# Self-attention logits from the normalised rows and one product of both weights, in a fused attention and feed-forward block

## The chip, the cores and the metric

The kernel runs on one core of a Trainium2 chip. A core has five engines that run side by side and meet at semaphores: TensorE (PE, matrix products into PSUM), VectorE (DVE), ScalarE (ACT), GpSimd (POOL) and SyncE (SP), which issues DMAs. ScalarE and GpSimd issue DMAs as well. The metric is the device time of one execution in microseconds; shown is the median of several runs. One further execution is recorded by the hardware profiler; its span runs from the first to the last instruction.

## The reference

There are 8 batches. `x` is [8, 128, 512], the context is [8, 2048, 384], everything is float32. Three layers follow one another, each added to `x`; a layer norm without gain stands ahead of each.

```python
x = x + xattn(layernorm(x), ctx)       # 8 heads of 64, 2048 context rows
x = x + attn(layernorm(x))             # one head of 512
x = x + ffn(layernorm(x))              # 512 -> 2048 -> 512, quantised

# attn(y), the layer that the change touches
queries = y @ Wq + bq
keys    = y @ Wk + bk
values  = y @ Wv + bv
logits  = einsum('bik,bjk->bij', queries, keys)
logits  = where(j > i, -inf, logits)
probs   = softmax(logits, axis=1) / sqrt(512)     # over the queries i
read    = einsum('bij,bjv->biv', probs, values)
return y + read
```

The softmax runs over the queries, and the layer adds its own input, the normalised rows, to its result. With y_i the row of the query and y_j that of the key, a logit is

```
(y_i Wq + bq) . (y_j Wk + bk) = y_i . (y_j Wk Wq^T + Wq bk) + y_j . (Wk bq) + bq . bk
```

so it can be formed from the rows themselves, the product Wk Wq^T (512 x 512), the vectors Wq bk and Wk bq, and one number.

## The kernel before

The kernel keeps tiles with 128 partitions. Rows and weights of 512 lie in NK = 4 blocks of 128. The 8 batches of the later layers are two groups of GB = 4, so that a matmul can move GT = 512 columns.

**Order of the work.** TensorE's order is the order of the source throughout (L136). So is ScalarE's and VectorE's (L242, L244) until `first.close()` and `in_turn.close()` at L781 and L782, in the first step of the last batch. What comes after that on VectorE and ScalarE, and all of GpSimd's and SyncE's work, DMA issues included, is put in order by a planner: it simulates the program, and lets an engine take the instruction that is ready and stands first in the source. A later instruction can so be placed well ahead of an earlier one that is not ready yet. A tile that takes over the buffer of an older tile waits until all readers and writers of the older one are done, DMAs among them.

**Prologue.** The first 56 us form the keys of batch 0's first half by plain matmuls, the layer norm of all rows for the cross-attention (`q_norm`), its queries (`q_proj`, kept in DRAM) and sums of context blocks and of weight blocks (`sum_half`, `sum_w`) for a block product that needs 20 matmul units in place of 24 (`block_product`, L286). `keep_rows` (L454) adds the bias `bo` to the rows on GpSimd and stores them. Then come `k_proj(0, 0, (1,))` and `v_proj(0, 0)` (L714, L715). `block_product` is a generator that stops twice on the way, so that other work can be set between its parts.

**Main loop.** For each batch b and step m of 4 (two heads a step): `scores(b, m)` (16 matmuls; VectorE copies them out of PSUM with a running maximum, L483), `attend` of the step before, a `unit` of other matmuls, the exponentials (L497), the 32 x 32 transposes on VectorE and 16 DMAs that finish the transposition (`turns`, L502 to L513). The `unit` forms keys and values for the next batch; in the last batch there is no next one, and it forms the self-attention of group 0: the queries in step 1 (L741), the keys in step 2 (L743), the weights in step 3. The tile of values for the second half, `v_proj(b, 1)`, has the tag "v1" in the pool `vp`; for batch 0 it is first written in step 0, by the ScalarE copy at L300.

**Self-attention.** `enter_self_attention` (L675) frees the context's tiles and loads the weights and biases on GpSimd's queue. The class `SelfAttention` (L587 on) has for each row block: `norm` (L597; statistics and scaling on VectorE, the square root on ScalarE, the addition to the residual on GpSimd, L124), `turn` (L600; four TensorE transposes and a ScalarE copy into `xt`), `turned_rows` (L603; queries or keys, [512 features, 512 rows], 16 matmuls in the source and 32 instructions in the profile, evicted by ScalarE with the bias, L613), `weights` (L623; logits with the key on the partition, mask, softmax), `values` and `read`. Group 0 is normalised and turned at the end of step 0 of the last batch (L785 to L787). Group 1 follows behind the loop (L790 to L804, L869 to L877).

**Feed-forward.** `quantize_w2` (L816) rounds w2 to a small format on VectorE, `hidden` (L831) forms and rounds the hidden rows, `output` and `finish` (L854, L861) the result.

## Time and profile before

| | |
|---|---|
| time, median of 3 runs | 1126.11 us (1125.96 to 1127.3) |
| time of the profiled execution | 1125.29 us |
| its span | 1123.5 us |
| mean granted TensorE clock | 0.997 |
| TensorE busy | 1107.7 us |
| VectorE busy | 823.3 us |
| ScalarE busy | 338.0 us |
| GpSimd busy | 233.2 us |
| `psq` (queries) of group 0, start to end | 847.1 to 861.1 us |
| `psq` and `psk` of group 1, start of the first to start of the logits | 922.95 to 952.21 us |
| last matmul of the kernel ends | 1115.9 us |

Times in the profile are microseconds from the start of the span. A line of the timeline gives the start, the length, the engine, the source line, the instruction, "written<-read" by tile names, the shape, how many instructions were merged (x32), and in brackets the idle time just before and what ended it. Matmuls are pipelined: the length of one overlaps the next, so the spacing of starts is what counts. A float32 matmul of 512 columns appears as two instructions. PEld are TensorE's weight loads beside the matmuls; SPq are DMA issues on SyncE's queue. In a table of DMA issues the last number is the median time from issue to landing.

### The profile page before, as it was taken

Reading aid. Unit: us, or ns where it says so; the run is one execution under the profiler, and the core shown is the slowest. Engines: PE = TensorE matmul, PEld = TensorE weight load, DVE = VectorE, ACT = ScalarE, POOL = GpSimd, SP = SyncE. Lnnn points to the kernel's source line nnn. Section 1 sums busy time; section 2 is a strip of 40 time slices with the busy share of each in tenths; the row PEclk is TensorE's granted clock in tenths of the full one; section 3 lists DMA queues with packets and bytes.
Section 4 is the critical chain, followed back from the end, with each engine's and each line's share of the span. In section 5 each row is a group of like instructions: output and inputs, shape, how many; then the busy total and the mean of one; then the engine's idle time right before and its main releaser. Section 6 shows DMA issues by size and latency. Waiting matters only on the chain.

```text
span 1123.5 us, 16786 instructions
## 1 busy us (share of the span) xinstructions
PE 1107.7 (99%) x6286; PEld 833.9 (74%) x6286; DVE 823.3 (73%) x1710; ACT 338.0 (30%) x531; POOL 233.2 (21%) x322
## 2 busy tenths in 40 slices
PE   9999999999999999999999999999999999999997
PEld 5487778788878877787888788777865544687775
DVE  5947777777767777777777677777795559767777
ACT  3323223233322222232333222222343322232221
POOL 0404401520450044006204500440030000000001
PEclk9999999999999999999999999999999999999999
DMA  8415535534654455355346544543383473000001
GB/s 290 177 50 129 132 76 141 150 76 92 156 146 100 108 141 142 78 138 151 75 94 156 136 101 101 151 126 76 89 259 75 109 239 113 1 1 20 10 10 38
DMA packets 48497, 125.12 MB, mean 111 GB/s; under 512 B 10384, under 2 KB 15520, under 8 KB 47520
## 3 DMA queue, kind: packets, MB, share of 16 engines
q1 hardware_dynamic: 46192, 117.48, 40.5%
q0 software_dynamic: 1360, 5.78, 1.6%
q8 instruction: 50, 0.82, 0.3%
q10 hardware_dynamic: 864, 0.79, 0.2%
q14 instruction: 31, 0.25, 0.1%
HBM read 49.03 MB, written 7.86 MB: 51 GB/s over the span
## 4 chain that ended last, share of the span: by engine, by line
PE 95%; DVE 3%; ACT 1%; issue 0%; DMA 0%; DVEq 0%; ACTq 0%
PE pv_z L403 21%; PE pk_z L380 19%; PE po L524 10%; PE sc L479 10%; PE ph L847 9%; PE pv_b L403 4%; PE pk_b L380 3%; PE psq L609 3%; PE psk L609 2%; PE py L562 2%; PE psv L650 2%; PE pq L447 2%; PE pf L856 2%; PE k L362 2%; PE pl L628 1%; DVE p L483 0%
## 5 line engine op out<-in xcount | busy, mean ns | idle before, releaser
L497 ACT ACTIVATE p<-p,nm 128x2048 f32<-128x2048 f32 x64 | 128.2, 2003 | 427.7 <-DVE nm L491 311.1
L510 DVE STREAM_TRANSPOSE p<-p 128x512 f32<-128x512 f32 x256 | 158.9, 679 | 84.0 <-ACT p L497 83.9
L483 DVE TENSOR_SCALAR_CACHE_REDUCE p<-sc 128x512 f32<-128x512 f32 x256 | 159.0, 686 | 29.5 <-PE sc L479 28.9
L403 PE MATMUL pv_z<-wv_sums,x 128*128 128x256 f32 x640 | 157.9, 382 | 0.0
L205 POOL TENSOR_TENSOR m<-x 128x256 f32<-128x256 f32 x70 | 51.1, 730 | 513.1 <-DMA x<-in_ctx_t_dram 467.1
L380 PE MATMUL pk_z<-x,wk_sums 128*128 128x256 f32 x600 | 149.7, 382 | 0.8 <-ACT kt L300 0.6
L403 PEld LDWEIGHTS pv_z<-wv_sums,x 128*128 128x128 f32 x640 | 120.6, 190 | 18.0 <-issue 1.5
L524 PEld LDWEIGHTS po<-pT,v 128*64 128x64 f32 x2048 | 111.2, 137 | 24.6 <-issue 21.5
L380 PEld LDWEIGHTS pk_z<-x,wk_sums 128*128 128x128 f32 x600 | 112.7, 190 | 19.8 <-issue 2.9
L479 PE MATMUL sc<-kt,q 64*128 64x512 f32 x512 | 119.9, 603 | 2.5 <-DVE p L483 2.5
L524 PE MATMUL po<-pT,v 128*64 128x128 f32 x2048 | 118.9, 274 | 0.3 <-issue 0.3
L847 PE MATMUL ph<-xf,w 128*128 128x256 f32 x512 | 111.3, 379 | 0.0
L403 PE MATMUL pv_z<-wv_sums,m 128*128 128x256 f32 x448 | 107.5, 380 | 0.2 <-ACT v L300 0.2
L847 PEld LDWEIGHTS ph<-xf,w 128*128 128x128 f32 x512 | 97.4, 190 | 13.7 <-issue 0.5
L380 PE MATMUL pk_z<-m,wk_sums 128*128 128x256 f32 x420 | 101.4, 380 | 0.0
L479 PEld LDWEIGHTS sc<-kt,q 64*128 64x128 f32 x512 | 47.3, 187 | 62.3 <-issue 53.6
L403 PEld LDWEIGHTS pv_z<-wv_sums,m 128*128 128x128 f32 x448 | 83.4, 190 | 13.0 <-issue 0.8
L380 PEld LDWEIGHTS pk_z<-m,wk_sums 128*128 128x128 f32 x420 | 79.2, 190 | 11.7 <-DVE kt L303 0.4
L300 ACT COPY v<-pv_z 128x512 f32<-128x512 f32 x112 | 62.8, 589 | 58.9 <-PE pv_z L403 58.9
L300 ACT COPY kt<-pk_z 128x512 f32<-128x512 f32 (+1 forms) x112 | 59.7, 558 | 58.0 <-PE pk_z L380 57.5
L205 POOL TENSOR_TENSOR x<-x 128x256 f32<-128x256 f32 x98 | 69.8, 730 | 0.8 <-DMA x<-in_ctx_t_dram 0.8
L303 DVE TENSOR_TENSOR v<-pv_z,v 128x512 f32<-128x512 f32 x96 | 63.2, 685 | 5.2 <-PE pv_z L403 5.2
(171 smaller groups left out, 1223.2 us busy)
## 6 DMA issues: line engine op xcount, KB each, us to landing
pT<-p SPq DMA_DIRECT2D x512, 128.0 KB, 2.4
x<-in_ctx_t_dram SPq DMA_DIRECT2D x45, 512.0 KB, 5.6
w<-in_w_t_dram SPq DMA_DIRECT2D x1, 4096.0 KB, 13.2
w2f<-in_w_t_dram SPq DMA_DIRECT2D x16, 256.0 KB, 2.7
x_in<-in_x_dram SPq DMA_DIRECT2D x8, 256.0 KB, 6.7
xd<-x_in SPq DMA_DIRECT2D x2, 1024.0 KB, 4.3
qd<-xq SPq DMA_DIRECT2D x8, 256.0 KB, 4.5
q<-qd SPq DMA_DIRECT2D x8, 256.0 KB, 3.3
```

Source lines behind the costliest of these rows:

```text
L205: eng.tensor_tensor(x_block(b, h, to), x_block(b, h, one), x_block(b, h, two), ALU.add if op == "+" else ALU.subtract,)
L300: nc.scalar.copy(outs[ij], views(ps))
L303: nc.vector.tensor_tensor(outs[to], views(ps), outs[other], op)
L380: nc.tensor.matmul(ps[:, ts(i, BK)], wk_sums[:, WSLOT[WAT[r]], f2, :], x_block(b, h, XAT[r]), start=start and i == 0, stop=True, skip_grou ...
L403: nc.tensor.matmul(ps[:, ts(t, 256)], x[:, ts(t, P)], wv_sums[:, WSLOT[WAT[r]], :], start=start and t == 0, stop=True, skip_group_check=True,)
L479: nc.tensor.matmul(pair[i], q[r, :], kts[b, m // 2][r, m % 2, ts(n, 512)], start=True, stop=True)
L483: nc.vector.tensor_scalar(p[:, :, i].rearrange("p g (t i) -> p t g i", i=SQ)[:, ts(n, Q)], pair[i].rearrange("p (t g i) -> p t g i", g=Q, ...
L497: nc.scalar.activation(p[:, :, i], p[:, :, i], AF.Exp, bias=nms[b, m][:, i : i + 1], scale=SCALE, accum_out=sums[b][:, h : h + 1],)
L510: nc.vector.transpose(p[:, g, i], p[:, g, i])
L524: nc.tensor.matmul(pos[b][h * DH : (h + 1) * DH, ts(m, P)].rearrange("p (a i) -> p a i", a=Q), v[:, jt % 8, ts(2 * m + h, DH)], turned_[b, ...
L609: nc.tensor.matmul(ps, weight[:, k, ts(m, P)], self.xt[:, k, :], start=(k == 0), stop=(k == NK - 1),)
L847: nc.tensor.matmul(ps[:, :n], w1[:, k, ts(c, P)], xt[:, k, at], start=(k == 0), stop=(k == NK - 1),)
```

## The change

The logits are formed from the rows. In place of queries and keys of each group there is `both`, the product Wk Wq^T, formed once by TensorE (`both_weights`, 16 matmuls in the source) in the last batch's step 1, and `keys(both)`, the rows times this product plus Wq bk (16 matmuls per group). The logits are these keys against the normalised rows `xt`. The part y_j . (Wk bq) + bq . bk, a number per key row, is formed on VectorE for each row block in `norm` (a product with the row `u` = Wk bq, summed along the row) and enters where the mask was added.

The product needs both weights with their columns on the partitions. They are turned in the prologue: both weights are loaded into a tile `w_sa` of the tag "v1", VectorE forms Wq bk and Wk bq from them (eight products summed along the row) and transposes them in place in blocks of 32 x 32 (eight instructions), and 32 DMAs of SyncE write them to DRAM with the blocks put in their turned places. Each DMA takes 32 partitions and writes 512 pieces of 32 floats. The products and transposes are set between the parts of `k_proj(0, 0, (1,))` and `v_proj(0, 0)`. The bias rows go through DRAM to be spread over all partitions, on GpSimd's queue; the two bias tiles use the buffers of the tag "t", one of which `bo` has.

In the last batch, `norm` and `turn` of group 0 move from the end of step 0 to the end of step 1, behind the product. `enter_self_attention` loads the turned weights, Wk first, and the row `u` in place of the bias columns.

```diff
--- before.py
+++ after.py
@@ -275,6 +275,53 @@
     bo = tmp.tile([P, D], F32, tag="t", name="bo")
     nc.sync.dma_start(bo, xa_bo.partition_broadcast(P))
 
+
+    w_sa = vp.tile([P, 2, NK, D], F32, tag="v1", name="w_sa")
+    side = const.tile([P, 2, NK], F32, tag="side", name="side")
+    both_biases = const.tile([P, 1], F32, tag="both_biases", name="both_biases")
+    turned_w = [dram.tile([D, D], F32, tag=f"tw{i}", name=f"tw_{i}") for i in range(2)]
+
+    def across(v, n, name):
+
+        line = dram.tile([1, D], F32, tag=f"line{n}", name=f"line_{n}")
+        nc.gpsimd.dma_start(line.rearrange("o (k p) -> p (o k)", p=P), v)
+        return line[0].partition_broadcast(P)
+
+    for i, a in enumerate((sa_wq, sa_wk)):
+        nc.sync.dma_start(w_sa[:, i], a.rearrange("(k p) n -> p k n", p=P))
+    bias_rows = []
+    for n, a in (("bk", sa_bk), ("bq", sa_bq)):
+        c = const.tile([P, NK], F32, tag=f"c{n}", name=f"c_{n}")
+        nc.gpsimd.dma_start(c, a)
+        t = tmp.tile([P, D], F32, tag="t", name=f"row_{n}")
+        nc.gpsimd.dma_start(t, across(c, n, n))
+        bias_rows.append(t)
+
+    unread = ps_acc.tile([P, D], F32, tag="po", name="unread")
+
+    def dot(to, one, two):
+        nc.vector.scalar_tensor_tensor(unread, one, 1.0, two, ALU.mult, ALU.mult, accum_out=to)
+
+    def weight_by_bias(i):
+
+        for k in range(NK):
+            dot(side[:, i, k : k + 1], w_sa[:, i, k], bias_rows[i])
+
+    def turn_weight(i, ks):
+
+        for k in ks:
+            nc.vector.transpose(w_sa[:, i, k], w_sa[:, i, k])
+
+    def keep_weights():
+        for i in range(2):
+            for k in range(NK):
+                for a in range(Q):
+                    to = turned_w[i][:, k * P + a * SQ : k * P + (a + 1) * SQ]
+                    nc.sync.dma_start(
+                        to.rearrange("(g i) j -> i g j", i=SQ),
+                        w_sa[ts(a, SQ), i, k].rearrange("p (g j) -> p g j", j=SQ),
+                    )
+
     wk4 = wk.rearrange("p k (f j n) -> p k f j n", f=2, j=2)
     wv3 = wv.rearrange("p k (j n) -> p k j n", j=2)
     wk_sums = wxa.tile([P, len(WSLOT), 2, P], F32, tag="wk_sums", name="wk_sums")
@@ -589,36 +636,54 @@
 
         def __init__(self, g, pool, w):
             self.g, self.pool = g, pool
-            self.swq, self.swk, self.swv, self.bq, self.bk, self.bv, self.mask = w
+            self.swq, self.swk, self.swv, self.u, self.bv, self.mask = w
+            self.c = {}
             self.rows = [g * GB + i for i in range(GB)]
             self.xt = pool.tile([P, NK, GT], F32, tag="xt", name=f"xt_{g}")
             self.xn, self.es, self.vals = {}, {}, None
 
         def norm(self, b):
             self.xn[b] = normed(b, self.pool, "xn", GB, "s", add_to=True)
+            c = small.tile([P, 1], F32, tag="sc", name=f"sc_{b}", bufs=GB)
+            unread = self.pool.tile([P, D], BF16, tag="unread", name=f"unread_{b}")
+            nc.vector.scalar_tensor_tensor(
+                unread, self.xn[b], 1.0, self.u, ALU.mult, ALU.mult, accum_out=c
+            )
+            nc.vector.tensor_tensor(c, c, both_biases, ALU.add)
+            self.c[b] = c
 
         def turn(self, b):
             turned_into(self.xt, b, self.xn[b], "s")
 
-        def turned_rows(self, n, weight, bias):
-            t = self.pool.tile([P, NK, GT], F32, tag=f"s{n}", name=f"s{n}_{self.g}")
-            setattr(self, f"{n}t", t)
+        def both_weights(self):
+
+            self.both = self.pool.tile([P, NK, D], F32, tag="sq", name="both")
             for m in range(NK):
-                ps = bank(f"ps{n}_{self.g}_{m}")
+                ps = bank(f"psw_{m}")
                 for k in range(NK):
                     nc.tensor.matmul(
-                        ps, weight[:, k, ts(m, P)], self.xt[:, k, :],
+                        ps, self.swk[:, k, ts(m, P)], self.swq[:, k, :],
                         start=(k == 0), stop=(k == NK - 1),
                     )
-                nc.scalar.activation(t[:, m, :], ps, AF.Identity, bias=bias[:, m : m + 1])
+                nc.scalar.copy(self.both[:, m, :], ps)
                 if m == 1:
                     yield
 
-        def queries(self):
-            all_of(self.turned_rows("q", self.swq, self.bq))
-
-        def keys(self):
-            all_of(self.turned_rows("k", self.swk, self.bk))
+        def keys(self, both):
+
+            self.kt = self.pool.tile([P, NK, GT], F32, tag="sk", name=f"sk_{self.g}")
+            for m in range(NK):
+                ps = bank(f"psk_{self.g}_{m}")
+                for k in range(NK):
+                    nc.tensor.matmul(
+                        ps, both[:, k, ts(m, P)], self.xt[:, k, :],
+                        start=(k == 0), stop=(k == NK - 1),
+                    )
+                nc.scalar.activation(
+                    self.kt[:, m, :], ps, AF.Identity, bias=side[:, 0, m : m + 1]
+                )
+                if m == 1:
+                    yield
 
         def weights(self, b):
 
@@ -626,11 +691,13 @@
             ps = bank(f"pl_{b}")
             for k in range(NK):
                 nc.tensor.matmul(
-                    ps[:, :S], self.kt[:, k, ts(i, S)], self.qt[:, k, ts(i, S)],
+                    ps[:, :S], self.kt[:, k, ts(i, S)], self.xt[:, k, ts(i, S)],
                     start=(k == 0), stop=(k == NK - 1),
                 )
             lg = self.pool.tile([P, S], F32, tag="lg", name=f"lg_{b}", bufs=2)
-            nc.vector.tensor_tensor(lg, ps[:, :S], self.mask, ALU.add)
+            nc.vector.scalar_tensor_tensor(
+                lg, ps[:, :S], self.c[b], self.mask, ALU.add, ALU.add
+            )
             nm = small.tile([P, 1], F32, tag="snm", name=f"snm_{b}", bufs=4)
             nc.vector.reduce_max(nm, lg, axis=AX.X, negate=True)
             e = self.pool.tile([P, S], F32, tag="e", name=f"e_{b}", bufs=4)
@@ -676,11 +743,13 @@
         src.close()
         wsa = ctx.enter_context(tc.tile_pool(name="wsa", bufs=1, reuse_waits="tile"))
         sap = ctx.enter_context(tc.tile_pool(name="sap", bufs=1, reuse_waits="tile"))
-        w = [
-            load_w(wsa, a, NK, n, nc.gpsimd)
-            for a, n in ((sa_wq, "swq"), (sa_wk, "swk"), (sa_wv, "swv"))
-        ]
-        w += [load_columns(wsa, sa_bq, "bq"), load_columns(wsa, sa_bk, "bk")]
+        w = []
+        for i, n in ((1, "swk"), (0, "swq")):
+            w.insert(0, load_w(wsa, turned_w[i], NK, n, nc.gpsimd))
+        w.append(load_w(wsa, sa_wv, NK, "swv", nc.gpsimd))
+        u = wsa.tile([P, D], F32, tag="u", name="u")
+        nc.gpsimd.dma_start(u, u_line)
+        w.append(u)
         w.append(load_row(wsa, sa_bv, "bv"))
 
         mask = wsa.tile([P, P], F32, tag="mask", name="mask")
@@ -711,8 +780,18 @@
     for g in range(NG):
         keep_rows(g)
     load_q(0)
+    dot(both_biases, bias_rows[0], bias_rows[1])
+    weight_by_bias(0)
     all_of(k_proj(0, 0, (1,)))
-    all_of(v_proj(0, 0))
+    weight_by_bias(1)
+    u_line = across(side[:, 1], "u", "u")
+    turn_weight(0, range(2))
+    values = first_of(v_proj(0, 0))
+    first_of(values)
+    turn_weight(0, range(2, NK))
+    turn_weight(1, range(NK))
+    keep_weights()
+    all_of(values)
     next_half(1, 0)
 
     wo = load_w(wop, xa_wo, NK, "wo", nc.sync, tag="wq")
@@ -738,9 +817,9 @@
             elif not last:
                 unit = k_proj(b + 1, m - 2)
             elif m == 1:
-                unit = sa0.turned_rows("q", sa0.swq, sa0.bq)
+                unit = sa0.both_weights()
             elif m == 2:
-                unit = sa0.turned_rows("k", sa0.swk, sa0.bk)
+                unit = sa0.keys(sa0.both)
             else:
                 for r in sa0.rows:
                     sa0.weights(r)
@@ -782,9 +861,10 @@
                     in_turn.close()
                     sap, w = enter_self_attention()
                     sa0 = SelfAttention(0, sap, w)
-                    for r in sa0.rows:
-                        sa0.norm(r)
-                        sa0.turn(r)
+            if last and m == 1:
+                for r in sa0.rows:
+                    sa0.norm(r)
+                    sa0.turn(r)
     for r in sa0.rows:
         sa0.values(r)
     sa1 = SelfAttention(1, sap, w)
@@ -866,8 +946,7 @@
         add.tensor_tensor(y, y, xs[b][:, cols], ALU.add)
         nc.sync.dma_start(out[b][:, cols], y)
 
-    sa1.queries()
-    sa1.keys()
+    all_of(sa1.keys(sa0.both))
     for r in sa1.rows:
         sa1.weights(r)
     for r in sa1.rows:
```

## The prediction

> **What bounds the kernel now.** I read the page first: TensorE is busy nearly the whole span and carries 95% of the chain that ended last, at the full clock.
>
> ```profile
> span 1123.5 us, 16786 instructions
> PE 1107.7 (99%) x6286; PEld 833.9 (74%) x6286; DVE 823.3 (73%) x1710; ACT 338.0 (30%) x531; POOL 233.2 (21%) x322
> ...
> PE 95%; DVE 3%; ACT 1%; issue 0%; DMA 0%; DVEq 0%; ACTq 0%
> ```
>
> So a matmul that goes away is worth its full spacing, and work put on another engine is free until it makes TensorE wait. Next the waits of TensorE and its timeline in the two places where the change removes something.
>
> ```profile
> PE sc L479 <- DVE p L483: 2.5, 1, 2.5
> ...
> 834.42 1.91 PE L131 MATMUL pt_s<-ident,xn_s 128*128 128x128 f32 x16
> 836.26 3.70 PE L479 MATMUL sc<-kt,q 64*128 64x512 f32 x14
> 842.41 1.12 PE L479 MATMUL sc<-kt,q 64*128 64x512 f32 x2 [2.45 <-DVE p L483]
> ...
> 922.95 15.70 PE L609 MATMUL psq<-xt,swq 128*128 128x512 f32 x32 [0.68 <-ACT xt L132]
> 938.48 13.90 PE L609 MATMUL psk<-xt,swk 128*128 128x512 f32 x32
> 952.21 4.11 PE L628 MATMUL pl<-sq,sk 128*128 128x128 f32 x32
> ```
>
> A projection is 32 instructions here (16 in the source), start to start 952.21 - 938.48 = 13.73 us. The query projection of group 1 took 15.53 because the granted clock was 0.5 for 3.4 us after the idle gaps at 920 to 923. Last, the prologue, where the change adds: VectorE, the first ScalarE write into the tile that will be shared, and SyncE's queue.
>
> ```profile
> 59.26 0.42 DVE L306 TENSOR_TENSOR kt<-kt,pk_z 128x256 f32<-128x256 f32 x1 [3.58 <-ACT kt L300]
> ...
> 70.57 0.69 DVE L306 TENSOR_TENSOR v<-v,pv_z 128x512 f32<-128x512 f32 x1 [4.51 <-ACT v L300]
> 72.55 0.69 DVE L303 TENSOR_TENSOR v<-pv_b,v 128x512 f32<-128x512 f32 x1 [1.29 <-PE pv_b L403]
> 76.00 0.69 DVE L303 TENSOR_TENSOR v<-pv_b,v 128x512 f32<-128x512 f32 x1 [2.76 <-PE pv_b L403]
> ...
> 98.40 0.58 ACT L300 COPY v<-pv_z 128x512 f32<-128x512 f32 x1 [3.75 <-PE pv_z L403]
> ...
> 82.90 1.28 SPq L166 DMA_DIRECT2D x<-in_ctx_t_dram  x3
> 100.12 10.10 SPq L513 DMA_DIRECT2D pT<-p  x16
> ...
> L461 SPq DMA_DIRECT2D q<-qd x8: 577/578/644, 47.2 to 681.6; - x8
> ...
> q<-qd SPq DMA_DIRECT2D x8, 256.0 KB, 3.3
> ```
>
> **The change, part by part.** Everything is summed against the profiled execution's own 1125.29 us (span 1123.5 and 1.79 around it), which lies 0.82 under the median of 1126.11.
>
> *Projections.* Four of them become three (the product of the weights, and the keys of both groups): -13.73 us. In group 0 the product takes the place of the queries one for one, so the gain appears behind 923 us, in group 1. The half-clock stretch does not go with the queries: the gap before it comes from row 7's norm, which stays, so the keys inherit it.
>
> *Norms of the last batch.* Moved past them on TensorE: 16 transposes (1.84 us, no saving) now stand behind the product instead of ahead of the scores of step 1. No DMA moves with them, nothing moves on SyncE; on GpSimd the four row additions may come later, and the load of the row `u` takes the slot of the two bias columns. The 2.45 us wait at 842 had one cause: VectorE normalised rows 4 to 6 there (three instructions in 4.10 us beside GpSimd's additions) ahead of the first reduction of the scores, at 841.66. Those norms reuse the buffers of rows 0 to 3, which are now transposed only behind the product, so they cannot be placed there: -2.45. The other end: the new dot products on VectorE need `u`. Its neighbour `bv` was issued at 833.70 and took 7.5 us, so `u`, issued at 832.6 in the slot of `bq`, lands near 840. If the planner, which orders VectorE from here on, sets one ahead of the reductions, they start at 840.1 plus one to four dots of 0.69, up to 842.9 against 841.66, and the wait stays or grows by 1.2. Between -2.45 and +1.2 I take -2.45: rows 0 to 3 must be normalised first and the reductions come earlier in the program.
>
> *The product needs both weights early.* They landed 10.3 and 16.3 us after issues at 812.9 and 813.6, so by 830; the product starts at about 842. Cost 0; without this cover it would wait for the DMA.
>
> *VectorE in the prologue.* Nine dots (one for both biases, eight for the weights) at the 0.61 us spacing of the reductions of L483, also 128x512, and eight transposes at 4.86/8 = 0.61. Five dots fit in the idle 3.58 us before 59.26 (5 x 0.61 = 3.05); four dots and two transposes in the 4.51 before 70.57 (3.66); the other six transposes (3.66) run from 71.3 to 74.9, so the operation of 72.55 is 2.4 late and is done before the one of 76.00 is ready, which waits for TensorE. Cost 0, from the idle time alone. The first dot also needs the second bias row, whose buffer is that of `bo`: free when GpSimd ends L456 at 26.89 + 12.57 = 39.5, plus a slow landing of 7.5, 47, ahead of 55.7.
>
> *Loads of the two weights, 2 MB.* They follow `bo` on SyncE at 18.6. The engines moved about 385 GB/s until 26, then had nothing until 33.86; 2 MB is 5.4 us. Cost 0.
>
> *Turned weights to DRAM.* 32 DMAs on SyncE, each 512 pieces of 128 bytes. The tile they read is the one that the second half of the values writes first at 98.40, so ScalarE waits for the last landing, and TensorE behind it within a microsecond, since the accumulation goes on in the same bank. The first transposes are done at 66.1 + 6 x 0.61 = 69.8. No row has a 128-byte store to DRAM. The nearest is the load of `q`: also 512 pieces per DMA, 0.578 us of issue, and 3.3 us to landing. At this pace the last one lands at 69.8 + 32 x 0.578 + 2.7 = 91.0, 7.4 us early: cost 0. The upper row: in the packet records each 512-byte piece of `q` occupied one of the 16 engines for 28 ns; 32 pieces per engine are 0.90 us per DMA, the end 101.3, the wait 2.9. I take 0, as issue was the longer of the two for this shape when loads came alone, and keep 2.9. Behind these on SyncE stand the loads of batch 1: issued at 89 instead of 82.9, GpSimd's sums end at 102.3 + 6 = 108, needed at 121.1: hidden. The transposed probabilities at 100.12 are not touched.
>
> The DMA page of the Trainium skill ("DMA: Bandwidth & Descriptors", Specifications) speaks against this step: transfers under 512 bytes are read, modified and written. No run here shows it. As an estimate, a piece then costs two 512-byte ones, 56 ns, 1.8 us per DMA, the last landing at 130, and the sum would be some 15 us above today's instead of below.
>
> *VectorE around the feed-forward part.* The keys come 13.73 us sooner, but the quantisation of w2 still fills VectorE until 968. From 968 to 1003 it was busy 22.22 of 35 us: 12.8 us of cover for 13.73 plus one dot of row 7, 0.69. Short by 1.6 us. If the late work is the quantisation of the hidden tile, nobody waits (0); if it is the norms of rows 4 to 7 behind one tile of 5 us, TensorE waits 6.6. I take 1.0, near the low end, since two tiles and seven PSUM banks stand between them. The logits' addition keeps its shape (0.28); the other seven dots fall into VectorE's waits for scores.
>
> Sum: 1125.29 - 13.73 - 2.45 + 0 + 0 + 1.0 = 1110.1, and 0.82 more for the median: 1110.9, rounded to 1111.
>
> The second rule is on the clock: "TensorE: Matmul & The Clock Gate" (Why this matters for your kernels) warns of gaps over about 3 us. The trace is stricter: 2.46 us of idle in two pieces at 920 to 923 did halve the clock, 2.45 us at 840 did not. By the page the half clock at 923 would go, and the sum be 1.7 lower; by the row it stays.
>
> **The rivals.**
> *Stores so slow that the change loses (slower).* The place is the write at 98.40, the price 32 us per microsecond of a DMA beyond 0.81. It decides where the wait eats 16.2: (98.4 + 16.2 - 2.7 - 69.8) / 32 = 1.32 us per DMA, 41 ns per piece. The 1024-byte pieces of `w_in` took 46 ns; at that price the last lands at 69.8 + 47.1 + 2.7 = 119.6, the wait is 21.2, and the time 1132. For it: the pieces are stores at a pitch of 2 KB, which no row shows. Against it: 46 ns is for eight times the bytes.
> *Stores in between.* 0.81 to 1.32 us per DMA: 1111 to 1127, middle 1118.
> *VectorE gives part back.* The dots wait for `u` ahead of the reductions (+3.65) or the late norms hold TensorE (+5.6): 1115 to 1120. For it: VectorE is busy 25.59 of the 26 us from 927 to 953 and GpSimd's contention tripled three of its instructions at 838. Against: all its idle time after 968.
>
> **How the numbers follow.** The forecast's case 0.50 (own range 1107 to 1115: half clock gone -1.7, the 1.0 not paid, the store bound +2.9), stores in between 0.17, VectorE 0.15, slow stores 0.18. A measurement of this kernel tells 0.2% (2.3 us) from no change, so faster is below 1123.9. Three quarters of the in-between case lie below it: 0.50 + 0.13 + 0.15 = 0.78; 0.03 within; 0.19 slower (slow stores and the in-between case's end). The range 1107 to 1124 holds 0.50 + 0.13 + 0.15 less a little at its ends, leaving out the slower cases.
>
> **What would show it.** No psq in group 1 and the logits 13.7 us closer to row 7's transposes; no wait of the scores near 842; VectorE's 70 to 76 us full without a wait of TensorE; SyncE issuing 32 stores from 70 to 89 and ScalarE's write at 98.40 in its place. It is wrong if ScalarE waits there for a DMA, if a dot stands before the reductions at 836, or if the transposes pt_f at 989 wait for VectorE.

## The result, and the profile after

| | before | after |
|---|---|---|
| time, median of 12 runs | 1125.87 us (1124.87 to 1127.30) | 1125.83 us (1122.39 to 1130.87) |
| time of the profiled execution | 1125.29 us | 1124.47 us |
| its span | 1123.5 us | 1122.7 us |

The ratio is 0.9998 with a 95% interval of 0.9986 to 1.0011: no change where 15 us less were forecast. The times after scatter over 8.5 us, those before over 2.4.

The page of the kernel after, its span, the busy time of each engine, and the shares of the chain that ended last by engine:

```profile
span 1122.7 us, 16820 instructions
PE 1098.4 (98%) x6254; PEld 830.2 (74%) x6254; DVE 844.1 (75%) x1760; ACT 334.7 (30%) x527; POOL 236.1 (21%) x328
...
PE 88%; DVE 7%; DMA 3%; issue 1%; ACT 0%; SPq 0%; ACTq 0%; DVEq 0%
```

TensorE lost the 32 matmuls and 9 us of busy time, but its share of the chain fell from 95% to 88%: VectorE and the DMAs now stand in it. The waits of TensorE after (what waited, for whom; sum in us, times, longest):

```profile
PE pk_z L427 <- DVE kt L353: 4.9, 1, 4.9
PE sc L526 <- DVE p L530: 2.5, 1, 2.5
PE early L255 <- POOL ident masks.py:199: 2.4, 1, 2.4
PE pv_z L450 <- DVE v L353: 1.8, 1, 1.8
...
PE sc L526 <- DVE rows L612: 1.3, 1, 1.3
```

Of these, before had the second (2.5) and 1.4 of the third. Where they stand on TensorE's timeline after (start, duration, instruction, the wait ahead of it):

```profile
67.90 1.22 PE L427 MATMUL pk_z<-x,wk_sums 128*128 128x256 f32 x2 [4.93 <-DVE kt L353]
...
123.11 1.99 PE L450 MATMUL pv_z<-wv_sums,x 128*128 128x256 f32 x8 [1.79 <-DVE v L353]
...
845.70 2.85 PE L526 MATMUL sc<-kt,q 64*128 64x512 f32 x12
849.85 1.12 PE L526 MATMUL sc<-kt,q 64*128 64x512 f32 x2 [1.31 <-DVE rows L612]
853.48 2.07 PE L526 MATMUL sc<-kt,q 64*128 64x512 f32 x2 [2.50 <-DVE p L530]
...
937.70 14.00 PE L678 MATMUL psk<-xt,both 128*128 128x512 f32 x32 [0.67 <-ACT xt L132]
951.54 4.11 PE L693 MATMUL pl<-xt,sk 128*128 128x128 f32 x32
```

The gain is there: in group 1 a single projection stands between row 7's transposes and the logits, and they start 951.54 - 937.70 = 13.84 us after it. But everything ahead of it came late. Starts of the same instructions of TensorE in the two profiled executions, after less before:

| up to | late by | step added | what added it |
|---|---|---|---|
| first key blocks, 58.49 against 56.50 | 1.99 | +1.99 | 0.75 until the first key matmul, 1.24 in the first 40 of them |
| first value blocks, 74.89 against 65.44 | 9.45 | +7.46 | the wait of 4.93 at 67.90, half clock behind it |
| scores(0,1), 125.04 against 113.83 | 11.21 | +1.76 | the wait of 1.79 at 123.11 |
| scores(7,0), 816.65 against 805.46 | 11.19 | 0.0 | nothing, the main loop |
| group 1's first projection, 937.70 against 922.95 | 14.75 | +3.56 | the waits of 1.31 and 2.50 against one of 2.45 before, and 2.2 of half clock behind them |
| group 1's logits, 951.54 against 952.21 | -0.67 | -15.42 | 13.73 for the projection, 1.7 for the half clock that stood at 923 before |

From there to the end nothing moves: the last matmuls start 0.68 earlier than before, and the span is 0.8 shorter. So 14.75 us were lost in four places, and the gain of 15.42 paid for them. That the two come out alike is chance.

**What makes the prologue late.** The DMAs of the first 40 us after: bandwidth of 40 slices of 1 us, then transfers by tile with their median time from issue to landing.

```profile
GB/s 0 34 168 222 360 357 387 379 207 155 234 210 109 139 70 70 88 94 301 401 410 391 316 80 107 221 207 240 164 209 197 250 274 371 375 408 404 395 395 373
...
x_in<-in_x_dram SPq DMA_DIRECT2D x8, 256.0 KB, 13.0
...
wq<-in_xa_wq_dram SPq DMA_DIRECT2D x1, 1024.0 KB, 19.0
...
line_bk<-c_bk POOLq DMA_DIRECT2D x1, 2.0 KB, 9.5
...
line_bq<-c_bq POOLq DMA_DIRECT2D x1, 2.0 KB, 11.7
```

Between 10 and 18 us the engines move 70 to 234 GB/s; before they moved 182 to 410 there, the rows of x landed in 6.7 us and wq in 8.3. What is new in this stretch is the way of the two bias rows on GpSimd's queue: 2 KB each that take 10 and 12 us to land, because `across` writes a line to DRAM in 512 pieces of 4 bytes. VectorE's statistics of group 1 then start at 29.38 instead of 21.85, behind a wait of 4.47 us for x, and everything that VectorE does ahead of the first key products moves with them. VectorE after, where it makes TensorE wait:

```profile
63.65 0.69 DVE L303 SCALAR_TENSOR_TENSOR unread<-row_bk,row_bq 128x512 f32<-128x512 f32 x1
...
67.43 0.41 DVE L353 TENSOR_TENSOR kt<-kt,pk_z 128x256 f32<-128x256 f32 x1
...
118.70 3.16 DVE L384 TENSOR_TENSOR v<-v 128x512 f32<-128x512 f32 x1
...
844.17 4.37 DVE L118 TENSOR_SCALAR xn_s<-rows,mv_s,rs_s 128x512 f32<-128x512 f32 x2
...
852.12 0.68 DVE L649 SCALAR_TENSOR_TENSOR unread<-xn_s,u 128x512 bf16<-128x512 f32 x1
...
852.73 0.69 DVE L530 TENSOR_SCALAR_CACHE_REDUCE p<-sc 128x512 f32<-128x512 f32 x1
```

The sums of the value weights end at 63.65 (55.6 before), the five dots take 0.79 each, and the first addition to the keys comes at 67.43 instead of 59.26. At 118.70 an addition of 0.69 takes 3.16: GpSimd sums a context half beside it. At 852 two dots stand ahead of the first reduction of the scores. Less the 11.19 us that were lost by then, that reduction starts at 841.54, against 841.66 before: it did not come earlier. TensorE did: its 16 transposes stand behind the product now, so it reached these scores at 845.70 - 11.19 = 834.51 instead of 836.26, and waited longer. SyncE's queue after tells why GpSimd is at work at 118:

```profile
79.15 22.46 SPq L320 DMA_DIRECT2D tw<-w_sa  x32
101.72 1.41 SPq L166 DMA_DIRECT2D x<-in_ctx_t_dram  x3
```

The load of x(1,0) was issued at 82.90 before and is issued at 101.72 now, behind the 32 stores.

### The profile page after: what moved, and what is told of

Read it like the earlier page. It is cut to its first block, busy times and chain, and to the rows that moved or that the text cites. A ratio compares the mean times of both kernels' runs of the same rounds, so it can differ in the third digit from the quotient of the medians.

```text
span 1122.7 us, 16820 instructions
## 1 busy us (share of the span) xinstructions
PE 1098.4 (98%) x6254; PEld 830.2 (74%) x6254; DVE 844.1 (75%) x1760; ACT 334.7 (30%) x527; POOL 236.1 (21%) x328
## 4 chain that ended last, share of the span: by engine, by line
PE 88%; DVE 7%; DMA 3%; issue 1%; ACT 0%; SPq 0%; ACTq 0%; DVEq 0%
PE pv_z L450 20%; PE pk_z L427 19%; PE po L571 11%; PE sc L526 10%; PE ph L927 9%; PE pv_b L450 3%; PE pk_b L427 3%; PE psk L678 2%; PE psv L717 2%; PE py L609 2%; PE pf L936 2%; DMA x<-in_ctx_t_dram 1%; PE psw L664 1%; DVE m L205 1%; DMA x_in<-in_x_dram 1%; DVE x L205 1%
```

## The experiments

The theory after the two traces: the product of the weights gains what was forecast, and three things take it back: (1) the lines written in pieces of 4 bytes hold up the loads of the prologue, about 8 us; (2) the dots push the turning and its stores back and these the load of x(1,0), about 2 us; (3) at scores(7,1) the dots replace the wait that was to go. The rivals: the turning and its stores, the loads of 2 MB, or the dots as such cost the prologue; or the product gains less than its matmuls. The kernel before ran on the same chip in each set (medians 1124.98, 1127.22, 1125.56 and 1127.05); ratios are to it, with 95% intervals.

**The product alone.**

```diff
-        nc.sync.dma_start(w_sa[:, i], a.rearrange("(k p) n -> p k n", p=P))
...
-        nc.gpsimd.dma_start(t, across(c, n, n))
...
-    weight_by_bias(0)
...
-    keep_weights()
...
-            lg, ps[:, :S], self.c[b], self.mask, ALU.add, ALU.add
+            lg, ps[:, :S], self.mask, ALU.add
...
-            w.insert(0, load_w(wsa, turned_w[i], NK, n, nc.gpsimd))
+            w.insert(0, load_w(wsa, (sa_wq, sa_wk)[i], NK, n, nc.gpsimd))
```

> The product alone: nothing is added to the prologue, the weights are loaded unturned and the bias terms of the logits are left out (zero), so the time is that of the matmuls and the moved norms. Theory (a projection is worth its spacing and the rest of the change gives it back): psq of group 1 gone, 13.7 us, and at most 2.5 for the scores' wait: 1108 to 1111 us. Rival (the gain is lost in the feed-forward part, where VectorE falls behind): 1115 or more.

1111.46 us, 0.9879 (0.9864 to 0.9893), 13.5 us less than before and 0.5 above the expected range. The term of -13.73 was right, and nothing downstream took any of it: the logits of group 1 start at 938.01 instead of 952.21, and this lead of 14.2 us is also that of the span (1109.3 against 1123.5). Of it, 1.7 are half clock that is gone at 923, and 1.2 were lost at scores(7,1). TensorE still waited 0.77 + 1.37 us at scores(7,1), with no dot in the kernel, so part of what is lost there is neither the dots' nor the product's.

**The bias rows straight from DRAM** (later called rows_direct). They are given in their own order, and one transfer spreads each over the partitions.

```diff
-        c = const.tile([P, NK], F32, tag=f"c{n}", name=f"c_{n}")
-        nc.gpsimd.dma_start(c, a)
         t = tmp.tile([P, D], F32, tag="t", name=f"row_{n}")
-        nc.gpsimd.dma_start(t, across(c, n, n))
+        nc.gpsimd.dma_start(t, a.partition_broadcast(P))
```

> Both bias rows are loaded straight from DRAM, one broadcast DMA each, instead of column load, write of 512 single floats to DRAM, and broadcast load. All else is the changed kernel. Theory 1 (the bias rows' way through DRAM holds up the DMA engines in the prologue): the rows of group 1 and the context land as in the kernel before, the statistics of group 1 start near 22 us instead of 29.4, VectorE reaches the first key operation at 60 or earlier instead of 67.4, the wait of TensorE of 4.9 us and the half clock behind it go: 1117 us. Rival (the added instructions of VectorE or the 2 MB of weights in w_sa make it late): the wait stays near 5 us, 1124 to 1126.

1117.97 us, 0.9931 (0.9909 to 0.9953). The wait of 4.93 is gone and the first key blocks start at 56.91. What stays are a wait of 2.67 in the second value blocks and 1.3 + 2.56 at scores(7,1).

**The same chain of transfers in larger pieces.** This separates the pieces from the chain. The load of the column changes with the write of the line, from 128 pieces of 16 bytes to 4 of 512.

```diff
-        c = const.tile([P, NK], F32, tag=f"c{n}", name=f"c_{n}")
-        nc.gpsimd.dma_start(c, a)
+        c = const.tile([NK, P], F32, tag=f"c{n}", name=f"c_{n}")
+        nc.gpsimd.dma_start(c, a.rearrange("(k p) -> k p", p=P))
+        line = dram.tile([1, D], F32, tag=f"line{n}", name=f"line_{n}")
+        nc.gpsimd.dma_start(line.rearrange("o (k p) -> (o k) p", p=P), c)
...
-        nc.gpsimd.dma_start(t, across(c, n, n))
+        nc.gpsimd.dma_start(t, line[0].partition_broadcast(P))
```

> The changed kernel in which the bias rows still take three transfers each on GpSimd's queue (SBUF, line in DRAM, row), in the same order, but the line is written in 4 pieces of 512 bytes instead of 512 pieces of 4 bytes. Theory A (the 4-byte pieces occupy the DMA engines and hold up the loads of x and wq): the prologue is back where it was, landing of the x rows near 6.7 us, and the time is that of the kernel with the rows loaded straight, 1118 (1116 to 1120). Theory B (any chain of transfers ahead of others on GpSimd's queue does it, whatever the pieces): 1125 to 1126, as the changed kernel.

1116.73 us, 0.9912 (0.9895 to 0.9929). The DMAs of its first 40 us, as shown for the kernel after:

```profile
GB/s 0 14 185 242 355 352 384 357 211 127 220 358 391 404 403 393 387 387 406 389 418 399 406 391 387 385 389 387 387 389 395 160 51 8 188 451 410 0 35 223
...
x_in<-in_x_dram SPq DMA_DIRECT2D x8, 256.0 KB, 7.3
...
wq<-in_xa_wq_dram SPq DMA_DIRECT2D x1, 1024.0 KB, 8.8
```

The same three transfers for each row, the same 2 MB of weights behind them, and the bandwidth stays at 385 to 418 GB/s until 31 us. So it is the small pieces and not the chain. (That a line in pieces of 4 bytes does harm without a column load beside it shows below, at the line for u.) The 1.07 us before the first matmul stay here (its wait is 2.4 as after, against 1.4 with the rows loaded straight): the first transfer on GpSimd's queue is issued ahead of the identity that TensorE waits for.

**The chain alone, in the kernel before.** Its rows are read by nobody.

```diff
+    for n, a in (("bk", sa_bk), ("bq", sa_bq)):
+        c = const.tile([P, NK], F32, tag=f"c{n}", name=f"c_{n}")
+        nc.gpsimd.dma_start(c, a)
+        t = tmp.tile([P, D], F32, tag="t", name=f"row_{n}")
+        nc.gpsimd.dma_start(t, across(c, n, n))
```

> The kernel before with nothing of the change but the six transfers of the two bias rows through DRAM, which nobody reads. Theory A (these transfers cost the prologue by themselves, by holding up the x rows, wq and the weights of the value projection): the sums of wv end some 8 us later and the time is 1125 + 7 = 1132 (1130 to 1134). The rival (the prologue is late because of the nine dots, the turning and the 2 MB of weights): 1125 to 1127.

1135.10 us, 1.0079 (1.0064 to 1.0095): six transfers of 0.5 MB in all, without a reader, cost 7.9 us by the medians and 8.9 by the ratio, somewhat more than expected. The wait is the same one as after:

```profile
PE pk_z L393 <- DVE kt L319: 4.1, 2, 3.9
```

The rows of x land in 13.6 us here and wq in 17.7. Together with the run before this settles (1): undone, it gives 7.5 to 9.7 us back (0.9998 - 0.9931 and 0.9998 - 0.9912 of 1126); done alone, it takes 7.9 to 8.9.

**The turning alone, in the kernel before.** Loads of both weights, 32 turns, 32 stores, no reader.

```diff
+    for i, a in enumerate((sa_wq, sa_wk)):
+        nc.sync.dma_start(w_sa[:, i], a.rearrange("(k p) n -> p k n", p=P))
...
+    turn_weight(0, range(2))
+    values = first_of(v_proj(0, 0))
...
+    keep_weights()
```

> The kernel before with the turning alone: both weights of self-attention loaded into v1's place, their 32 turns on VectorE and the 32 stores to DRAM, which nobody reads; no bias rows, no dots, no product. Theory (the stores do not delay the write of v1, but they push the load of x(1,0) on SyncE's queue from 83 to 88 us or later, so that GpSimd's 20 sums run beside VectorE's additions in the second value projection): one wait of 1.8 to 2.7 us at that projection, 1125.6 + 2.3 = 1127.9 (1127 to 1129). The rival of the prediction (slow stores hold v1's write, which stands at 98 us): over 1130. That the turning costs nothing: 1125 to 1126.5.

1126.83 us against 1127.05, 1.0003 (0.9992 to 1.0014): nothing, and my 2.3 us were wrong. SyncE's queue, of this kernel and then of the one with the rows loaded straight:

```profile
67.38 18.47 SPq L293 DMA_DIRECT2D tw<-w_sa  x32
85.95 1.40 SPq L166 DMA_DIRECT2D x<-in_ctx_t_dram  x3
```

```profile
70.11 23.19 SPq L318 DMA_DIRECT2D tw<-w_sa  x32
93.40 1.41 SPq L166 DMA_DIRECT2D x<-in_ctx_t_dram  x3
```

With the turning alone the stores start 2.7 us earlier and take 4.7 us less, x(1,0) comes only 3 us later than before, and no wait appears. The 2.7 us are the dots' doing: with the rows loaded straight the last four of them run from 66.39 to 69.38, ahead of the first transposes. The 4.7 us are not. Just ahead of the first store, GpSimd's queue writes the line for `u` to DRAM, which is again 512 pieces of 4 bytes. Here are this DMA and the times from issue to landing of the 32 stores with the rows loaded straight, then those times with the turning alone:

```profile
L287 POOL DMA_DIRECT2D line_u<-side x1: 772/772/772, 69.8 to 69.8; - x1
...
DMA to landing us min/median/max: 1.9/2.0/10.2
```

```profile
DMA to landing us min/median/max: 1.8/2.0/2.8
```

Beside the line the first nine stores, issued from 70.1 to 77.9, land after 4.6 to 10.2 us, and issuing one of them takes up to 3.12 us, where 0.50 is the median. From 74 to 80 us the DMA engines are full and move 30 to 55 GB/s, against 118 to 122 with the turning alone. So late, the stores end at 93.3, GpSimd's sums last until 113 and meet VectorE's additions (4.04 instead of 0.69), and TensorE waits 2.67. Thus the stores alone are free; the dots ahead of them and, for the larger part, the line for `u` beside them make them late enough. No run takes away one of the two without the other.

**The load of x(1,0) past the stores.** It is issued on ScalarE's queue, everything else as with the rows loaded straight.

```diff
+        eng = nc.scalar if (b, h) == (1, 0) else nc.sync
...
-            nc.sync.dma_start(
+            eng.dma_start(
```

> rows_direct, and the three loads of batch 1's first context half are issued by ScalarE, so they no longer stand behind the 32 stores on SyncE. Theory (the stores delay these loads, GpSimd's sums run later and hold one VectorE addition of the values for 3.16 us): the sums start within 6 us of the end of the values' matmuls, the addition takes 0.7 us, the wait of 1.8 us at the end of the second half of the values goes: 1.8 us less than rows_direct. Rival: the wait has another cause, no difference to rows_direct.

1117.42 us, 0.9924 (0.9908 to 0.9941): not told apart from the kernel without it. The old wait went and another came. ScalarE's first write into v1:

```profile
102.29 1.07 ACT L346 COPY v<-pv_z 128x512 f32<-128x512 f32 x2 [6.95 <-DMA tw<-w_sa]
```

Beside 1.5 MB of context and the line for `u` the 32 stores took 30.1 us, and the write that shares their tile waited 6.95 us for the last of them. This is the place of the rival that I had called slow stores; it opens only once another load is set beside them.

**The weights given turned.** With the rows loaded straight; turns and stores go, the dots stay.

```diff
-    turn_weight(0, range(2))
...
-    keep_weights()
...
-            w.insert(0, load_w(wsa, turned_w[i], NK, n, nc.gpsimd))
+            w.insert(0, load_w(wsa, (sa_wq_t, sa_wk_t)[i], NK, n, nc.gpsimd))
```

> The kernel with the bias rows loaded straight, and in addition the two weights for the product are given turned, so that the 32 turns and the 32 stores go (the dots and the loads that feed them stay). Theory (the stores on SyncE's queue push the load of the next context half back, GpSimd's sums then run beside VectorE's additions in the second value projection, and TensorE waits 2.7 us there): that wait goes, x(1,0) is issued near 83 us, and the time is 1118.0 - 2.7 = 1115.3 (1114 to 1117). The rival (the wait is the dots' or the late prologue's, not the stores'): 1117 to 1119.

1116.77 us, 0.9908 (0.9889 to 0.9927). The wait of 2.67 is gone and x(1,0) is issued at 84.22, as expected; the time fell by only 1.2 (2.6 by the ratios, as the two ran on different chips), inside the scatter of both. In the two profiled executions the rest went to half clock in other places: the first 40 key matmuls took 18.68 instead of 17.62 and group 1's keys 15.70 instead of 14.00.

**The number per key row left out.** It is the same for all entries of one softmax, so it cancels. The row u, one bias row and five of the nine dots of the prologue go with it, and the eight later ones.

```diff
-    dot(both_biases, bias_rows[0], bias_rows[1])
-    weight_by_bias(1)
-    u_line = across(side[:, 1], "u", "u")
...
-            lg, ps[:, :S], self.c[b], self.mask, ALU.add, ALU.add
+            lg, ps[:, :S], self.mask, ALU.add
```

> rows_direct, and the number per key row is left out: it is the same for all queries of a key, so the softmax over the queries cancels it. Gone with it are the row u and its DMAs, the second bias row, five dots in the prologue and the eight in the norms. Theory (the dots that wait for u ahead of the reductions make the wait at the scores of step 1): that wait falls to 1 us or less, 1113 us. Rival (the norms of rows 2 and 3 beside GpSimd's additions make it): 2 us or more stay, 1115 to 1117.

1113.59 us, 0.9891 (0.9875 to 0.9908), 4.4 below the kernel with the rows loaded straight. The line for `u` is gone as well: the stores run from 68.03 to 86.4, the wait of 2.67 is gone, and at scores(7,1) the waits are 0.77 + 1.37 instead of 1.3 + 2.56. This is (2) and the dots' part of (3). The time is the theory's, but the 2.14 us that stay at scores(7,1) are the rival's sign: the dots are not all that holds the scores there.

**What holds scores(7,1).** The waits of 0.77 + 1.37 remain without any dot. Two things come into question: the norms, which the planner sets ahead of the reductions, or something else that ends at the same time. Three more kernels cross them. In all three the weights are given turned, the number per key row is left out, and the number per column is formed by TensorE.

The norms behind the reductions in VectorE's written order:

```diff
             scores(b, m)
+            if last and m == 1:
+                mvs = sa0.stats()
...
+                sa0.norms(mvs)
                 for r in sa0.rows:
-                    sa0.norm(r)
                     sa0.turn(r)
+                sa1.norm(sa1.rows[2])
+                first.close()
```

> Toward a better version: both weights given turned, no turning, no stores, no bias rows and no dots; the number per key row left out, which is the same for all entries of a softmax and cancels; the number per column formed by TensorE (16 products with one column each) after the product; the norms of group 0 behind the reductions of scores(7,1) in VectorE's written order. By the sum: product alone 1111.5, its wait at scores(7,1) of 2.1 and the half clock behind it (4.85 instead of 3.70) gone, 16 small products at 0.03 to 0.1 each added: 1108.9 (1107.5 to 1110.5). The rival (the half clock comes back at another place, or the norms are late for the turning at 862): 1111 to 1114.

1118.19 us, 0.9928 (0.9913 to 0.9942): a miss by 9 us. VectorE's first reduction of scores(7,1), then TensorE there, then the 16 DMAs of step (7,0)'s probabilities from issue to landing:

```profile
840.60 0.69 DVE L488 TENSOR_SCALAR_CACHE_REDUCE p<-sc 128x512 f32<-128x512 f32 x1 [5.05 <-DMA pT<-p]
```

```profile
841.36 2.07 PE L484 MATMUL sc<-kt,q 64*128 64x512 f32 x2 [2.90 <-DVE p L488]
...
862.92 3.63 PE L646 MATMUL pside<-bk,swq 128*128 128x1 f32 x32
```

```profile
DMA to landing us min/median/max: 4.8/7.3/9.7
```

With the norms out of the way VectorE stands idle for 5.05 us and starts no earlier (839.83 with the product alone). The reductions write the tile p, and step (7,0)'s DMAs still read it: they land after up to 9.7 us (2.2 to 2.4 a step earlier), while the rows (2 MB) and the three weights (3 MB) are loaded beside them; the DMA engines are full from 815 to 840. In the kernel before this was no hold yet. The last two of the 16 DMAs there, then here:

```profile
L513 SPq DMA_DIRECT2D pT<-p x2: 561/575/589, 831.2 to 831.8; - x2
...
DMA to landing us min/median/max: 4.7/4.8/4.9
```

```profile
L518 SPq DMA_DIRECT2D pT<-p x2: 589/590/592, 832.3 to 832.9; - x2
...
DMA to landing us min/median/max: 6.0/6.7/7.4
```

Before, they had landed by 836.7, some 5 us ahead of the first reduction at 841.66, and with the product alone by 836.7 against 839.83: there the norms held the reductions. Here the last one is issued 1.1 us later, behind the start of the load of `swv` (1 MB, 831.95), and lands at 840.3. And the 16 products of one column cost 3.63 us, not the 0.5 to 1.6 that I had set.

The three weights on SyncE's queue behind those DMAs, with the norms left free and with the norms behind the reductions:

```diff
-            w.insert(0, load_w(wsa, (sa_wq_t, sa_wk_t)[i], NK, n, nc.gpsimd))
-        w.append(load_w(wsa, sa_wv, NK, "swv", nc.gpsimd))
+            w.insert(0, load_w(wsa, (sa_wq_t, sa_wk_t)[i], NK, n, nc.sync))
+        w.append(load_w(wsa, sa_wv, NK, "swv", nc.sync))
```

> The same with the loads behind the stores, but the norms left where the planner puts them, ahead of the reductions. Theory of two holds: the loads alone bring little, since the norms still end near 840: the wait stays at 2.1 with its half clock, 1115 to 1117. The rival (the loads were the only hold, the norms merely stood there): as the kernel with both, 1111 to 1114.

> The kernel of the run before with weights given turned and the norms behind the reductions, and in addition the three weights of self-attention are loaded on SyncE's queue behind the stores of step (7,0) instead of on GpSimd's queue ahead of them. Theory (the first reduction of scores(7,1) waits for two things that end within a microsecond of each other, the norms on VectorE and the landing of step (7,0)'s p, which shares the DMA engines with 5 MB of loads; each alone hides the other): the wait of 2.90 and the half clock behind it (0.95 on scores, 2.08 on the attention product) go: 1118.2 - 5.9 = 1112.3 (1111 to 1114). The rival (the landing is not the loads' doing): 1117 to 1119.

1117.09 us, 0.9930 (0.9914 to 0.9947), with the loads moved alone, and 1113.63 us, 0.9893 (0.9877 to 0.9910), with both. VectorE up to the first reduction, and the landing, with the loads moved alone:

```profile
834.09 3.73 DVE L120 TENSOR_SCALAR xn_s<-rows,mv_s,rs_s 128x512 f32<-128x512 f32 x2
...
840.44 0.16 DVE L119 RECIPROCAL rs_s<-sd_s 128x1 f32<-128x1 f32 x1 [0.42 <-ACT sd_s L117]
840.87 0.69 DVE L488 TENSOR_SCALAR_CACHE_REDUCE p<-sc 128x512 f32<-128x512 f32 x1 [0.26 <-DMA swv<-in_sa_wv_dram]
```

```profile
DMA to landing us min/median/max: 2.7/2.9/3.1
```

VectorE is at the norms until 840.60. The 0.26 us behind them are put down to the load of `swv`, which the reduction does not read and which lands later (832.4 + 9.0 = 841.4). With both, the first reduction and TensorE:

```profile
835.70 0.69 DVE L488 TENSOR_SCALAR_CACHE_REDUCE p<-sc 128x512 f32<-128x512 f32 x1 [0.36 <-PE sc L484]
```

```profile
834.54 3.70 PE L484 MATMUL sc<-kt,q 64*128 64x512 f32 x16
838.18 3.71 PE L529 MATMUL po<-pT,v 128*64 128x128 f32 x64
```

Norms moved: 840.60. Loads moved: 840.87. Both: 835.70, and the 16 score matmuls run through without a wait. Either alone leaves the reductions where they were; it takes both. That the first two times lie within 0.3 us of each other is chance, since they come from two kernels; where neither was moved, the DMAs landed 3 to 5 us ahead of the reductions.

**The version that these point to.** Loads late, norms behind the reductions, no number per key row, weights given turned; the number per column by four dots on VectorE from one raw copy of Wq and one row loaded straight.

```diff
-    for i, a in enumerate((sa_wq, sa_wk)):
-        nc.sync.dma_start(w_sa[:, i], a.rearrange("(k p) n -> p k n", p=P))
+    nc.sync.dma_start(w_sa[:, 0], sa_wq.rearrange("(k p) n -> p k n", p=P))
```

> The better version with both: loads behind the stores, norms behind the reductions, and the number per column formed by four dots on VectorE (Wq loaded once more as it is, the row of one bias loaded straight) in place of the 16 products of one column on TensorE, which took 3.63 us. By the sum from the kernel with the product alone: 1111.5 less its wait of 2.14 and 1.15 of half clock behind it: 1108.2 (1106.5 to 1110). The rival (the early half of the kernel loses what the late half wins, as 1.1 us on the first key products with w_sa in flight): 1109 to 1111.

1106.77 us, 0.9839 (0.9822 to 0.9857), 18.8 us less than before, below the product alone and inside the expected range.

```profile
834.98 3.70 PE L508 MATMUL sc<-kt,q 64*128 64x512 f32 x16
838.61 3.71 PE L553 MATMUL po<-pT,v 128*64 128x128 f32 x64
```

## Why the prediction was wrong

*Projections, -13.73: right.* The product alone gave 13.5. That the half clock at 923 stays was wrong for this execution: group 1's keys took 14.00, and half clock stood at 67 (2.4 us) and at 855 (2.2) instead. The Trainium skill ("TensorE: Matmul & The Clock Gate", Why this matters for your kernels) warns of gaps over about 3 us. The half clock at 67 followed a gap of 4.93 us, as that has it. But the one at 855 followed gaps of 1.31 and 2.50, and gaps of 1.78 and 0.67 ahead of 937 were followed by none, while in the kernel before the same two gaps, at 920 to 923, were. Neither the page nor my stricter row decided it; the last section has more rows.

*VectorE in the prologue, "Cost 0, from the idle time alone": the step that failed, 7.46 us.* It counted the dots and asked when the second bias row lands. It never priced what the six transfers that bring the rows do to the loads beside them; that the lines are written in pieces of 4 bytes stood in the code. They cost 7.9 to 8.9 us by themselves, through the rows of x, for which VectorE waits (4.47 us) ahead of all its later work. A smaller error in the same term: a dot takes 0.79 from start to start where I took 0.61 from L483, so the five took 3.78 (63.65 to 67.43), more than the idle 3.58.

*Loads of the two weights, cost 0: right.* With the line in large pieces the 2 MB pass at 390 GB/s and no wait follows. *Turned weights to DRAM, cost 0: right as to the write of v1.* The stores alone were issued at 0.58 us each, as forecast, and cost nothing; after it was 0.70, since the first nine stood behind the line for `u`, and the write was not held even so. The Trainium skill's page "DMA: Bandwidth & Descriptors" (Specifications) says that transfers under 512 bytes are read, modified and written, from which I had estimated 1.8 us per DMA and a last landing at 130. The trace does not agree with that price for these pieces of 128 bytes: the last store is issued by 101.6, and the median one lands 2.1 us after its issue. For the pieces of 4 bytes the rule pointed the right way, and I did not hold it against them.

*"Behind these on SyncE stand the loads of batch 1 ... hidden": failed, 1.76 us.* I had the issue at 89 and the sums' end at 108, from a start at 69.8 and 0.578 per store. They started at 79.15, with the late prologue and behind the dots, and took 4 us longer beside the line for `u`, another transfer that the sum did not price; this put the issue at 101.72 and the sums' end at 121.3. Being done in time for their reader was not enough either: the sums ran beside VectorE's additions and stretched one from 0.69 to 3.16.

*Norms of the last batch, -2.45: failed, +3.56 in its place with the half clock.* That the wait at 842 had one cause, the norms, holds for the kernel before. What failed is that norms "cannot be placed there" and that "the reductions come earlier in the program". The norms of rows 4 to 6 did move, to 875 as forecast; the norms of rows 0 to 3, two of which took 4.37 us beside GpSimd, and two dots took their place ahead of the reductions, which began where they had begun. As TensorE arrived sooner, the wait grew by 1.36 (3.81 against 2.45), and 2.2 of half clock followed. Nor would moving the norms have been enough: the kernel that did so met the landing of p. The upper end that I kept, +1.2 for dots waiting for u, was the nearer one; u landed at 851.3, just as VectorE came free for the first dot, so the time went to what stood ahead and to the two dots and not to u.

*VectorE around the feed-forward part, +1.0: not paid.* The offset is the same from 951 to the end.

*The rivals.* "VectorE gives part back" had a part of scores(7,1), the dots ahead of the reductions, but not the norms of rows 0 to 3 beside them. It set 3.65 above the forecast; measured were 3.56 + 2.45 = 6.0, 2.2 of it half clock. None of the rivals held the one that mattered: that the prologue's DMAs, not its arithmetic, become late.

## What to carry to other kernels

Price every transfer of a change by its number of pieces and by who shares the DMA engines at that moment, not by its bytes or by its own reader's deadline: 2 KB in pieces of 4 bytes cost more here than 2 MB in rows. Before a wait is counted as gain, ask what would hold the engine next: a profile names the last release, and here the DMAs that had landed 3 to 5 us ahead of it became the hold as soon as the norms were moved. A term that a softmax cancels is better left out than placed: that was worth 4.4 us here.

## What the runs showed of the hardware that I had not expected

- **Pieces of 4 bytes.** Two lines of 512 such pieces cut the DMA engines from about 390 to 70 to 140 GB/s between 12 and 18 us, and the median landing of 256 KB loads on another queue rose from 6.7 to 13.0 us. A third line at 69.8 us held stores of another queue for up to 10.2 us instead of 2.8. Written in 4 pieces of 512 bytes, two lines did no such harm (7.3 us for the 256 KB loads). What the pieces do inside the DMA engines, no view shows.
- **GpSimd beside VectorE.** An addition of two tiles of 128 x 512 in SBUF took 3.16 and 4.04 us instead of 0.69 while GpSimd added tiles; its neighbours, which read one operand from PSUM, kept their 0.69.
- **A dot with its unread product in PSUM** took 0.79 from start to start (0.14 for reading the sum), the same dot with the product in SBUF as bf16 0.61 (0.08), followed there by a reduction and not by another dot. Which of these differences matters was not tried.
- **Products of one column** of 128 x 128 weights took 3.63 / 32 = 0.11 us each, so a matrix times a vector on TensorE cost a quarter of the product with 512 columns (14.00).
- **Half clock comes and goes.** After the same wait of 2.45 us at scores(7,1), the attention product behind it ran at full clock in the kernel before and with 1.7 us of half clock in the one with the turning alone:

```profile
843.46 3.71 PE L524 MATMUL po<-pT,v 128*64 128x128 f32 x64
```

```profile
843.65 5.38 PE L544 MATMUL po<-pT,v 128*64 128x128 f32 x64
```

In the second, group 1's queries took 14.00, in the first 15.70. The first 40 key matmuls took 17.43 to 18.84 in these profiles. The length of the idle time therefore did not decide it; what does, stays open. That this is also the scatter of 8.5 us after is likely, but only argued: the mean granted clock is 0.987 in the two longest of the twelve executions and 0.992 to 0.993 in the three shortest.
